# Sixteen word offsets for the split tiles of a float32r FFN, and a pad ahead of its second input

## The chip, the core and the metric

The kernel runs on one core of a Trainium2 chip. The metric is the device time of one execution in microseconds; before the change it is 880.83 us, the median of two runs (879.86 and 881.8).

## What is computed

One transformer block with attention and FFN in parallel, on x of shape (2, 2048, 256) in float32:

```python
xn = layernorm(x)
q, k, v = xn @ Wq, xn @ Wk, xn @ Wv
attn = softmax(where(causal, q @ k.T, -max) * 256 ** -0.5) @ v @ Wo
h = silu(xn @ w1.T * s1) * (xn @ w2.T * s2)      # 256 -> 1024
h = gelu(h @ h1.T * sh1)                         # 1024 -> 1024
h = gelu(h @ h2.T * sh2)                         # 1024 -> 1024
out = x + attn + h @ w3.T * s3                   # 1024 -> 256
```

The FFN's weights w1, w2, h1, h2 and w3 are ternary (-1, 0 or 1); the scales are vectors.

## The kernel before

**Stages.** The 4096 rows are cut into N = 8 blocks of TB = 512. Attention comes first and takes until about 285 us. It leaves two things in DRAM: xn of each block, transposed and split in two (`xT_d`), and the attention's result (`r_d`). Beside it, the ternary matrices are looked at, and the factors of h1 are made. A branch on `flag` then takes `ffn_ternary` (L671), which runs to the end; the other branch, `ffn`, is for weights that are not ternary and isn't run here.

**Splitting.** TensorE multiplies in the type float32r, which keeps fewer bits than float32. A value is therefore held as two float32r tiles side by side, the rounded value and the rest. `split` (L695) makes such a tile of [P, 2, TB], 4096 bytes per partition, from a pool of 16 buffers (`hp`, L678): ScalarE casts f into half 0 (L698), VectorE subtracts half 0 from f into half 1 (L699). Every product runs over both halves, `a` in (0, 1), and adds both into one PSUM bank. As the weights are small whole numbers, they need no such split.

**The FFN** takes two blocks at a time, four pairs in all. In each pair:

- `first` (L702) multiplies w1 and w2 with xn. The even block's xn lies in `xh0`, the odd block's in `xh1` (name xh1t). There are 16 steps of 8 matmuls (L715), each w [128 x 128] stationary and xn [128 x 512] moving. ScalarE takes silu (L720), VectorE multiplies (L721), and some of the results are split.
- `square` (L747) is called twice, for h1 and for h2. It is a Strassen-Winograd product: the 1024 x 1024 layer on two blocks is cut in 2 x 2, and seven products of half size stand for eight. `STEPS` (L39) names, for each, the factor of the weights and the set of four split tiles. `product` (L753) loads the factor from DRAM into one of three buffers of `wp`, and issues 4 x 4 x 2 = 32 matmuls (L763), w [128 x 128] stationary and a half of a split tile [128 x 512] moving. VectorE, ScalarE and GpSimd form the sums, the gelus and the next split tiles beside it.
- The output (L856 to L879), for the odd block and then for the even: `rest` gets `r_d` by DMA and x by another, added on GpSimd (L861). Then for each of four row tiles 16 matmuls (L871), now with the split tile [128 x 128] stationary and w3 [128 x 256] moving. VectorE scales (L877) and adds `rest` (L878) in a tile `y` of the pool `op` (L679, three buffers), and SP's queue stores it (L879).

**Order.** A scheduler places each engine's instructions when the program is built; within an engine they run in that order. SP's queue issues all the FFN's DMAs. The eight PSUM banks rotate through one pool. Pools are laid out in SBUF one after another in the order in which they are opened: first `const` with w1_sb, w2_sb, xh0, s3, the scales and `flag` (L113 to L118), then, once attention's pools are closed, `fwt` (w3_sb, xh1t), `wpt`, `stgpt`, `rawpt`, `hpt` and `opt`.

**Addresses in the built program**, in bytes in the partition, and what is left of them modulo 64: w1_sb 16512 (0), w2_sb 24704 (0), xh0 32896 (0), w3_sbt 42272 (32), xh1t 50464 (32), the three buffers of `wp` 58656, 66848 and 75040 (all 32), the 16 split tiles 150816 and on in steps of 4096 (all 32), attention's k, q, v and pT (all 32), wvo 48704 (0). A half of a split tile (2048 bytes), a column slice of w (512) and a c of xh (4096) are multiples of 64, so that these remainders hold for every operand.

Of the kernel before, what the change touches and what calls it, by code (L numbers as in the profile page):

```python
# [9 lines left out]
F32 = mybir.dt.float32  # L10
F32R = mybir.dt.float32r
# [9 lines left out]
P = 128  # L21
TB = 512
# [14 lines left out]


STEPS = [("A11", "B11"), ("S1", "T1"), ("S2", "T2"), ("S4", "B22"), ("S3", "T3"), ("A12", "B21"), ("A22", "T4")]  # L39
LOW_BITS = 0xFFF  # L40


# [20 lines left out]
def attn_ffn_kernel(  # L63
# [46 lines left out]
    const = ctx.enter_context(tc.tile_pool(name="const", bufs=1))  # L110
# [5 lines left out]
    s3 = const.tile([P, D], F32, name="s3")  # L116
    sc = {k: const.tile([P, HC], F32, name=f"{k}_s_sb") for k in ("w1", "w2", "h1", "h2")}
    flag = const.tile([1, 1], I32, name="flag")  # L118


    HB = H // 2
    HK = HC // 2
    factors = {k: dram.tile([P, len(STEPS), HK, HB], F32, name=f"factors_{k}") for k in ("h1", "h2")}

# [33 lines left out]
    with ExitStack() as actx:  # L158
# [311 lines left out]
        def score_steps(n, t):  # L470
            order = list(range(n - n % NB, n + 1))
            return [
                (6 * (TB if m < n else (t + 1) * P), lambda m=m: score(n, t, m, order))
                for m in order
            ]
# [41 lines left out]
        def look(src, dst):  # L517
            got = []

            def bits():  # L520
# [4 lines left out]
                with tc.issue_after(marks["DVE"]):  # L525
                    nc.vector.tensor_scalar(tb, tb, LOW_BITS, None, ALU.bitwise_and)
                with tc.issue_after(marks["ACT"]):
# [114 lines left out]
        while until < len(tiles) - 1:  # L642
# [7 lines left out]
            a = []  # L650
            if j < len(tiles):
                a = score_steps(*tiles[j])
                if j == 0:
                    a = []
            a = a + extra.get(j, [])
# [15 lines left out]
    def ffn_ternary(actx):  # L671
# [4 lines left out]
        stgp = actx.enter_context(tc.tile_pool(name="stgpt", bufs=2))  # L676
        rawp = actx.enter_context(tc.tile_pool(name="rawpt", bufs=25))
        hp = actx.enter_context(tc.tile_pool(name="hpt", bufs=4 * HK))  # L678
        op = actx.enter_context(tc.tile_pool(name="opt", bufs=3))  # L679
        ps = actx.enter_context(tc.tile_pool(name="pst", bufs=8, space=PSUM))  # L680

        w3_sb = fw.tile([P, HC, D], F32R, name="w3_sbt")
# [9 lines left out]
        def raw(name):  # L692
            return rawp.tile([P, TB], F32, tag="raw", name=name)

        def split(f, name):  # L695

            r = hp.tile([P, 2, TB], F32R, tag="h", name=f"h_{name}")
            nc.scalar.copy(r[:, 0, :], f)  # L698
            nc.vector.tensor_tensor(r[:, 1, :], f, r[:, 0, :].bitcast(F32), ALU.subtract)  # L699
            return r  # L700

        def first(n):  # L702
# [3 lines left out]
            for k in ("B11", "B12", "B22", "B21"):  # L706
                xh = xh1 if k[2] == "2" else xh0
                for i in range(HK):
                    o = i + (HK if k[1] == "2" else 0)
                    name = f"w_{n}_{k}_{i}"  # L710
                    p1, p2 = banks(name, 2)
                    for p, w in ((p1, w1_sb), (p2, w2_sb)):
                        for c in range(DC):
                            for a in range(2):
                                nc.tensor.matmul(  # L715
                                    out=p, lhsT=w[:, c, ts(o, P)], rhs=xh[:, c, a, :],
                                    start=(c == 0 and a == 0), stop=(c == DC - 1 and a == 1),
                                )
                    f = B[k][i] = raw(f"f_{name}")
                    nc.scalar.activation(f, p1, AF.Silu, scale=sc["w1"][:, o : o + 1])  # L720
                    nc.vector.scalar_tensor_tensor(  # L721
                        f, p2, sc["w2"][:, o : o + 1], f, ALU.mult, ALU.mult
                    )
                    if k == "B11":
                        sets[k].append(split(f, f"{n}_{k}_{i}"))
                    elif k == "B12":
                        t1(B, sets, f"{n}", i)
                    elif k == "B22":
                        b22(B, sets, f"{n}", i)
                if later and k in ("B11", "B12"):  # L730
                    later.pop(0)()
# [3 lines left out]
        def t1(B, sets, name, i):  # L735
            nc.vector.tensor_tensor(B["B11"][i], B["B12"][i], B["B11"][i], ALU.subtract)
            sets["T1"].append(split(B["B11"][i], f"{name}_T1_{i}"))

        def b22(B, sets, name, i):
            sets["B22"].append(split(B["B22"][i], f"{name}_B22_{i}"))  # L740
            nc.gpsimd.tensor_tensor(B["B12"][i], B["B22"][i], B["B12"][i], ALU.subtract)  # L741
            nc.vector.tensor_tensor(B["B22"][i], B["B22"][i], B["B11"][i], ALU.subtract)  # L742
# [4 lines left out]
        def square(layer, n, B, sets, last):  # L747
# [5 lines left out]
            def product(step, out, start):  # L753
                left, right = STEPS[step]
                w = wp.tile([P, HK, HB], F32R, tag="w", name=f"w_{name}_{left}")
                nc.sync.dma_start(
                    out=w.bitcast(F32).rearrange("p c o -> p (c o)"),
                    in_=factors[layer][:, step].rearrange("p c o -> p (c o)"),
                )
                for o in range(HK):  # L760
                    for c in range(HK):
                        for a in range(2):
                            nc.tensor.matmul(  # L763
                                out=out[o], lhsT=w[:, c, ts(o, P)], rhs=sets[right][c][:, a, :],
                                start=(start and c == 0 and a == 0), stop=(c == HK - 1 and a == 1),
                                skip_group_check=True,
                            )
                if later and step in (0, 2, 4, 5):
                    later.pop(0)()
# [77 lines left out]
        for n in range(0, N, 2):  # L847
# [8 lines left out]
            for m in (n + 1, n):  # L856
# [5 lines left out]
                h = sets["B11"] + sets["B21"] if m == n else sets["B12"] + sets["B22"]  # L862
# [164 lines left out]

    some = nc.values_load(flag[0:1, 0:1], min_val=0, max_val=LOW_BITS * SC * P)
    with tc.If(some == 0) as cmp:
        with ExitStack() as fctx:  # L1030
            ffn_ternary(fctx)
# [43 lines left out]
```

## Time and profile before

| | |
|---|---|
| median of the runs | 880.83 us |
| the profiled execution: time, and its span | 885.32 us, 883.4 us |
| granted TensorE clock, mean over the span | 0.992 |
| DVE, ACT, POOL busy | 70%, 56%, 29% |
| PE busy, its weight loads | 97%, 82% |
| start of the first L715, end of the last L871 | 285.6 us, 875.4 us |
| matmuls of L763, L715, L871 | 1792, 512, 512 |
| ACT cast L698, DVE subtract L699, x288 each | 0.62 us, 0.68 us (up to 2.8 us) |
| store of y, from issue to landing, x32 | 1.7 to 4.5 us, median 2.0 |

The span is from the first instruction of the profiled execution to its last. Busy time of PE counts a matmul from its start to its modelled end; neighbouring matmuls overlap, so that 97% doesn't say how fast they follow each other. That is read from the starts in the timeline, where a run of like instructions has one line with the start of the first, and the next line's start ends it.

### The profile page before, as it was taken

The numbers are of one execution on the slowest core, as the hardware profiler recorded it, in microseconds if no ns is written. First come the engines' busy times: TensorE is split into PE (matmuls) and PEld (weight loads), VectorE is DVE, ScalarE is ACT, GpSimd is POOL, SyncE is SP. The second block draws the span as 40 slices with busy tenths as digits, with TensorE's granted clock in tenths as the row PEclk, the third lists the DMA queues.
The fourth block names the chain that finished last, engine by engine and source line by source line (L and its number), as shares of the span: only waits on it lengthen the run. The fifth ranks groups of instructions, "written<-read, shape, count | busy, mean of one in ns | idle before, by whom it ended". The sixth has DMA issues, their size and how long they took to land.

```text
span 883.4 us, 12258 instructions
## 1 busy us (share of the span) xinstructions
PE 855.4 (97%) x4280; PEld 721.5 (82%) x4280; DVE 621.6 (70%) x1111; ACT 498.1 (56%) x881; POOL 258.4 (29%) x192
## 2 busy tenths in 40 slices
PE   8999889999998999999999999999999999999996
PEld 5988678888887878788988888888888898888886
DVE  6698667787763896786497596559568648848663
ACT  3456545755544655677256576626657635657670
POOL 4012835323211384440133051024115011502401
PEclk9999999999999999999999999999999999999999
DMA  8676699987882979844434444433444443144412
GB/s 268 243 224 200 195 313 298 343 298 207 294 253 58 377 256 343 294 143 143 137 102 144 143 143 144 155 109 118 143 142 144 143 144 96 48 143 144 143 48 76
DMA packets 63989, 162.51 MB, mean 184 GB/s; under 512 B 6704, under 2 KB 36528, under 8 KB 54704
## 3 DMA queue, kind: packets, MB, share of 16 engines
q1 hardware_dynamic: 60176, 149.07, 50.3%
q10 hardware_dynamic: 3744, 12.58, 5.0%
q8 instruction: 36, 0.59, 0.3%
q14 instruction: 33, 0.27, 0.1%
HBM read 113.92 MB, written 47.71 MB: 183 GB/s over the span
## 4 chain that ended last, share of the span: by engine, by line
PE 61%; DMA 4%; DVE 1%; POOL 1%; issue 0%; SPq 0%; POOLq 0%; DVEq 0%
PE ps_h_X L763 26%; PE ps_h_Z L763 13%; PE ps_w_B L715 10%; PE ps_h_Y L763 7%; PE ps_y L871 6%; DMA xt<-in_attn_x 2%; DMA w_h_A<-factors_h 1%; POOL rt L861 1%; DMA rt<-r_d 0%; DVE f_w_B L742 0%; DVE h_B L699 0%; POOL f_w_B L741 0%; DMA out<-yt 0%; DVE yt L878 0%; DVE yt L877 0%
## 5 line engine op out<-in xcount | busy, mean ns | idle before, releaser
L364 PE MATMUL pss<-k,q 128*128 128x512 f32 (+3 forms) x480 | 109.6, 369 | 3.7 <-ACT q L214 2.4
L364 PEld LDWEIGHTS pss<-k,q 128*128 128x128 f32 x480 | 82.3, 190 | 17.2 <-ACT q L214 2.7
L763 PE MATMUL ps_h_X<-h_h_T,w_h_S 128*128 128x512 f32 x384 | 89.0, 389 | 0.0
L443 PE MATMUL po<-v,pT 128*128 128x512 f32 x272 | 80.4, 407 | 6.5 <-ACT pT L423 5.8
L763 PEld LDWEIGHTS ps_h_X<-h_h_T,w_h_S 128*128 128x128 f32 x384 | 72.1, 188 | 15.0
L861 POOL TENSOR_TENSOR rt<-rt,xt 128x1024 f32<-128x1024 f32 x8 | 19.2, 2400 | 218.7 <-DMA rt<-r_d 212.1
L425 POOL TENSOR_TENSOR pT<-e,pT 128x512 fp32r<-128x512 f32 (+3 forms) x30 | 36.9, 1230 | 116.5 <-ACT pT L423 78.7
L784 ACT ACTIVATE k_h_u<-k_h_u,h_s_sb 128x512 f32<-128x512 f32 x64 | 46.3, 723 | 40.9 <-DVE k_h_u L783 40.7
L720 ACT ACTIVATE f_w_B<-ps_w_B,w_s_sb 128x512 f32<-128x512 f32 x64 | 43.0, 684 | 42.5 <-PE ps_w_B L715 42.5
L871 PEld LDWEIGHTS ps_y<-w_sbt,h_h_B 128*128 128x128 f32 x512 | 62.0, 192 | 0.3
L871 PE MATMUL ps_y<-w_sbt,h_h_B 128*128 128x256 f32 x512 | 62.1, 283 | 0.0
L715 PE MATMUL ps_w_B<-xh,w_sb 128*128 128x512 f32 x256 | 59.7, 390 | 1.3 <-DVE r L462 1.3
L715 PE MATMUL ps_w_B<-xh1t,w_sb 128*128 128x512 f32 x256 | 60.7, 397 | 0.0
L443 PEld LDWEIGHTS po<-v,pT 128*128 128x128 f32 x272 | 48.1, 192 | 15.0 <-ACT pT L423 6.7
L763 PE MATMUL ps_h_Y<-h_h_B,w_h_A 128*128 128x512 f32 x256 | 59.5, 389 | 0.6 <-DMA w_h_A<-factors_h 0.6
L763 PE MATMUL ps_h_X<-h_h_T,w_h_A 128*128 128x512 f32 x256 | 59.3, 389 | 0.0
L715 PEld LDWEIGHTS ps_w_B<-xh1t,w_sb 128*128 128x128 f32 x256 | 48.1, 188 | 12.0 <-ACT f_w_B L720 0.4
L715 PEld LDWEIGHTS ps_w_B<-xh,w_sb 128*128 128x128 f32 x256 | 47.8, 188 | 11.4 <-issue 1.5
L763 PEld LDWEIGHTS ps_h_Y<-h_h_B,w_h_A 128*128 128x128 f32 x256 | 48.0, 188 | 10.9 <-issue 1.0
L741 POOL TENSOR_TENSOR k_h_u<-k_h_p,k_h_u 128x512 f32<-128x512 f32 x16 | 24.3, 1526 | 110.0 <-ACT h_h_B L698 97.6
L763 PEld LDWEIGHTS ps_h_X<-h_h_T,w_h_A 128*128 128x128 f32 x256 | 48.1, 188 | 10.0
L385 ACT ACTIVATE s<-s,low 128x1024 f32<-128x1024 f32 (+7 forms) x48 | 43.0, 897 | 21.9 <-DVE low L379 21.8
(139 smaller groups left out, 1869.9 us busy)
## 6 DMA issues: line engine op xcount, KB each, us to landing
w_h_S<-factors_h SPq DMA_DIRECT2D x32, 1024.0 KB, 4.8
w_h_A<-factors_h SPq DMA_DIRECT2D x24, 1024.0 KB, 4.9
d<-b SPq DMA_DIRECT2D x18, 512.0 KB, 3.5
e<-d SPq DMA_DIRECT2D x72, 128.0 KB, 4.0
xT_d<-k SPq DMA_DIRECT2D x8, 1024.0 KB, 5.3
stg<-in_ffn_h_w ACTq DMA_DIRECT2D x16, 512.0 KB, 6.3
x<-in_attn_x SPq DMA_DIRECT2D x16, 256.0 KB, 5.3
r_d<-r SPq DMA_DIRECT2D x8, 512.0 KB, 5.8
```

The lines of the kernel that those rows point to most:

```text
L364: nc.tensor.matmul(out=ps[:, :w], lhsT=qs[n][:, c, a, ts(t, P)], rhs=ks[m][:, c, b, :w], start=(k == 0), stop=(m < n and k == 3 * DC - 1),)
L385: marks["ACT"] = nc.scalar.activation(st["s"][:, at], st["s"][:, at], AF.Exp, bias=low, accum_out=st["sums"][:, u // UK : u // UK + 1],).ins
L425: engine.tensor_tensor(lo, src, hi.bitcast(F32), ALU.subtract)
L443: nc.tensor.matmul(out=st["po"], lhsT=pT[:, 0, ts(j, P)], rhs=vs[m][:, j, :, :], start=(m == first and j == 0), stop=False,)
L715: nc.tensor.matmul(out=p, lhsT=w[:, c, ts(o, P)], rhs=xh[:, c, a, :], start=(c == 0 and a == 0), stop=(c == DC - 1 and a == 1),)
L720: nc.scalar.activation(f, p1, AF.Silu, scale=sc["w1"][:, o : o + 1])
L741: nc.gpsimd.tensor_tensor(B["B12"][i], B["B22"][i], B["B12"][i], ALU.subtract)
L763: nc.tensor.matmul(out=out[o], lhsT=w[:, c, ts(o, P)], rhs=sets[right][c][:, a, :], start=(start and c == 0 and a == 0), stop=(c == HK - 1 ...
L784: nc.scalar.activation(C[k][o], r[o] if r else banks[o], AF.Gelu, scale=s[:, at : at + 1])
L861: nc.gpsimd.tensor_tensor(rest, rest, xt, ALU.add)
L871: nc.tensor.matmul(out=ys[t][:, :D], lhsT=h[c][:, a, ts(t, P)], rhs=w3_sb[:, c, :], start=(c == 0 and a == 0), stop=(c == HC - 1 and a == 1),)
```

## The change

Three edits. A tile of 8 words per partition is added to the `const` pool, after `flag`. A split tile's buffer becomes 16 words longer, 4160 bytes, and the two halves lie in it from word 0, 1, 2, ... 15, 0, ... on, counted over all splits. The pool `op` has two buffers instead of three, which gives `y` two; `rest` and `xt` have one each by their own setting.

```diff
+SHIFTS = 16
...
     flag = const.tile([1, 1], I32, name="flag")
+    const.tile([P, 8], F32, name="pad")
...
-        op = actx.enter_context(tc.tile_pool(name="opt", bufs=3))
+        op = actx.enter_context(tc.tile_pool(name="opt", bufs=2))
...
+        splits = [0]
+
         def split(f, name):

-            r = hp.tile([P, 2, TB], F32R, tag="h", name=f"h_{name}")
+            t = hp.tile([P, 2 * TB + SHIFTS], F32R, tag="h", name=f"h_{name}")
+            r = t[:, ds(splits[0] % SHIFTS, 2 * TB)].rearrange("p (a t) -> p a t", a=2)
+            splits[0] += 1
             nc.scalar.copy(r[:, 0, :], f)
             nc.vector.tensor_tensor(r[:, 1, :], f, r[:, 0, :].bitcast(F32), ALU.subtract)
             return r
```

In the built program of the change w1_sb, w2_sb and xh0 stay where they were. Everything after `const` moves: w3_sbt, xh1t, the three buffers of `wp`, the 16 split buffers (now in steps of 4160), k, q, v and pT begin at a multiple of 64, wvo at 32 past one. A split tile's two halves lie at its word offset past a multiple of 64. PE, ACT, POOL and SP have the same instructions in the same order; on VectorE, L877 and L878 of the later output tiles of a pair stand one to three places further back.

## The prediction

> **What bounds the kernel now.** I read the share of each engine first, then the chain that ended last, then the waits of PE in the FFN, then the starts of its matmuls in the timeline. The share and the chain on the page:
>
> ```profile
> PE 855.4 (97%) x4280; PEld 721.5 (82%) x4280; DVE 621.6 (70%) x1111; ACT 498.1 (56%) x881; POOL 258.4 (29%) x192
> ...
> PE ps_h_X L763 26%; PE ps_h_Z L763 13%; PE ps_w_B L715 10%; PE ps_h_Y L763 7%; PE ps_y L871 6%; DMA xt<-in_attn_x 2%; DMA w_h_A<-factors_h 1%; POOL rt L861 1%; DMA rt<-r_d 0%; DVE f_w_B L742 0%; DVE h_B L699 0%; POOL f_w_B L741 0%; DMA out<-yt 0%; DVE yt L878 0%; DVE yt L877 0%
> ```
>
> 62% of the span stands on the chain as FFN matmuls (26+13+10+7+6). The waits of PE between 294 and 884 us are two, both in the first pair of blocks:
>
> ```profile
> PE ps_h_X L763 <- DVE f_w_B L721: 2.2, 1, 2.2
> PE ps_h_Y L763 <- DMA w_h_A<-factors_h: 0.6, 1, 0.6
> ```
>
> So from 285.6 us (first L715) to 875.4 us (end of L871) PE waits 2.8 us for anything with a name, and the FFN's time is the number of its matmuls times the distance from one start to the next. That distance, not the mean duration (389 ns at L763, which overlaps), is the number to read. Timeline of PE, second pair of blocks; the columns are start in us, length in us, engine, line:
>
> ```profile
> 443.03 15.15 PE L715 MATMUL ps_w_B<-xh1t,w_sb 128*128 128x512 f32 x64
> 458.02 7.44 PE L715 MATMUL ps_w_B<-xh,w_sb 128*128 128x512 f32 x32
> 465.30 7.46 PE L763 MATMUL ps_h_X<-h_B,w_h_A 128*128 128x512 f32 x32
> 472.60 7.42 PE L763 MATMUL ps_h_Z<-h_T,w_h_S 128*128 128x512 f32 x32
> ```
>
> Starts differ by 14.99 us for the 64 matmuls on xh1t: 234.2 ns each. The 32 on xh take 7.28 us: 227.5 ns. The chain of work has the products of L763 at 7.25 us each throughout, 226.6 ns a matmul. These are matmuls of one size, none waiting. What differs is the place of the operands. In the built program w1, w2 and xh0 start at a multiple of 64 bytes; xh1t, the split tiles and the factors in wp all start 32 bytes (8 words) past one. Moving and stationary operand are therefore 0 words apart (modulo 16) at L763 and in L715 on xh, and 8 apart in L715 on xh1t. Apart by 0, 226.6 to 227.5; apart by 8, 234.2.
>
> Apart by 0 isn't enough, though. In attention k and q are also 0 apart, yet runs of 12 that wait for nothing go slower:
>
> ```profile
> 200.01 2.93 PE L364 MATMUL pss<-k,q 128*128 128x512 f32 x12
> 202.78 0.64 PE L448 MATMUL po<-v,pT 128*128 128x256 f32 x4
> ...
> 228.85 2.91 PE L364 MATMUL pss<-k,q 128*128 128x512 f32 x12
> 231.60 0.39 PE L443 MATMUL po<-v,pT 128*128 128x512 f32 x1
> ```
>
> 2.77 and 2.75 us for 12: 230.8 and 229.2 ns. Read start by start, such runs step irregularly between 224 and 240 ns, while L763 after at most some ten irregular steps repeats 227, 227, 226 to its end. I read this as settling: where every pair of operands has the same offset, the starts fall into a rhythm at 226.6; where not, they wander at 230 to 234.
>
> **What the Trainium skill says.** "TensorE: Matmul & The Clock Gate", Back-to-back issue gap, prices a warm matmul at N/2.4+2.5 ns, 215.8 for 512 columns; this trace shows 226.6 at best over a product, 10.8 more. The same page (Part 2, step 1) says that PE has two separate SBUF read ports, so that loading the next weights doesn't steal bandwidth from the running matmul; 234.2 against 227.5 for an offset alone speaks against full independence. "SBUF — State Buffer", Operand start alignment, lets a 4-byte operand start at any word and says of it "This is about legality, not speed". So the 16 words are allowed and unpriced. Its Specifications give 16-byte cachelines with a penalty for each crossing; no run here shows it.
>
> **The change part by part.** On PE, ACT, POOL and SP the instructions and their order are the same; on DVE only the last output tiles of each pair move. What changes is addresses.
>
> 1. *The pad* moves everything after the const pool by 32 bytes. xh1t comes to 0 apart from w1 and w2: 256 matmuls (64 in each of four pairs) from 234.2 to 227.5, 6.7 ns each: -1.7 us. In attention q, k, v and pT move together and wvo stays 8 words from k: nothing.
>
> 2. *The split tiles at L763.* The factors are now at 0 and the r-th split lies at word r mod 16. A pair's splits come in sets of four, so a product of 32 matmuls meets four neighbouring offsets, two matmuls each, and over the products all 16 come about equally often. The trace prices two of the sixteen: 0 (226.6) and 8 (234.2). Straight between them around the circle, the mean distance from 0 is 4 words, which gives 230.4. The runs that never settle give 229 to 231 at offset 0 itself. I take 231: 4.4 ns by 1792 matmuls (14 products of 32 in each pair, four pairs) = +7.9 us. Bounds: below, 224, the shortest step seen, -4.7 us; above, all at 234.2, +13.6 us.
>
> 3. *The split tiles at L871* are the stationary operand, 256 columns. Starts are 119.9 ns apart (420.54 to 435.89 us for 128). pv in attention, 8 apart, 24 of 256 columns from 195.37 to 198.25 us, has 120.0. Nothing; at best about -1 us (512 by 2 ns).
>
> 4. *Writing them.* The 288 splits (72 a pair) are an ACT cast (620 ns) and a DVE subtract (680 ns undisturbed). No such write off a 32-byte boundary is in the trace. During the products DVE is busy 66% (252.9 of 381 us in four windows), so a slower write hides there; before the first product it is busy 92% (24.78 of 27 us). Below: nothing, since the amount of data is equal. Above: 10% on 16 subtracts there, 1.1 us in each pair, +3 us after the first pair. I take 0.
>
> 5. *Two y buffers instead of three.* L877 of tile 2 now waits for tile 0 to be stored. The end of the kernel:
>
> ```profile
> 875.50 1.09 DVE L878 TENSOR_TENSOR yt<-yt,rt 128x256 f32<-128x256 f32 x3 [1.52 <-POOL rt L861]
> 875.95 3.24 SPq L879 DMA_DIRECT2D out<-yt  x4
> 877.78 0.42 DVE L877 TENSOR_TENSOR yt<-ps_y,s 128x256 f32<-128x256 f32 x1 [1.19 <-DMA out<-yt]
> 878.23 0.42 DVE L878 TENSOR_TENSOR yt<-yt,rt 128x256 f32<-128x256 f32 x1
> ```
>
> POOL ends the sum of rest late, three L878 follow, and tile 3 waits for tile 0's store until 877.78. After the change tile 2 waits for that same store and tile 3 for the next: four DVE operations instead of two stand after 877.78, +2 x 0.43 = +0.9 us, on the path that sets the end. At the three earlier pair ends the same wait holds L721 of the next pair behind it on DVE, and so the PSUM banks that L715 wants; two or three banks are still free there and PE shows no wait, so nothing; without that cover 3 x 0.9 us.
>
> Sum: -1.7 + 7.9 + 0 + 0 + 0.9 = +7.1 us. The profiled execution has a span of 883.4 us and a time of 885.32, so span 890.5; against the median of 880.83 us, 4.5 below that execution's time, 887.9.
>
> **Rivals.** *A, the rhythm holds whatever the offset.* Neighbouring offsets shift a start by a word (0.4 ns), which the rhythm may absorb. For it: after waits, L763 always returned to 226.6. Against: xh1t never does in 64 matmuls. Time: 880.83 - 1.7 + 0.9 = 880.0. *B, faster: other offsets keep the two reads out of each other's way.* For it: 10.8 ns a matmul over the skill's price have to come from something, and steps of 224 exist. Against: in the runs read they are single steps followed by long ones. At 224: 880.0 - 4.7 = 875.3. It turns faster than before where L763 falls below 227. More than 2% (17.6 us) would need 217.3. *C, over 2% slower: starts inside a 32-byte group cost more than any offset seen.* Place: 14 of 16 offsets at L763. Price: at 240, the longest step seen, 13.4 ns by 1568 = +21 us, 901. It decides from a mean of 236.9 at L763. Against: moving words are consecutive wherever they begin.
>
> **How the numbers follow.** The wandering rhythm 0.57, with its own range 884 to 894 (L763 at 228.8 to 234.2); A 0.17; B 0.16; C 0.10. Forecast 888. The range 874 to 897 holds the first, A, most of B, and part 4 at its upper bound; C lies outside. Over 2%, about what a measurement of this kernel can tell from no change: slower 0.10 (C), faster 0.03 (the far end of B), within 0.87.
>
> **What would show it.** Right: xh1t's 64 in 14.6 us; products of 7.3 to 7.5 us instead of 7.25, longer for sets whose words lie near 8; y's last L877 later by 0.9 us. Wrong: products all at 7.25 (A), below (B), or above 7.6 (C); L699 longer than 0.68 us where POOL is idle; a new PE wait at L715.

## The result and the profile after

The changed kernel takes 893.56 us (median of 893.36 and 893.75) against 880.83 us: ratio 1.0144, 95% interval 1.0095 to 1.0194, 12.7 us more (8.4 to 17.1). Its profiled execution has a time of 893.36 us and a span of 891.6 us.

From the page of the changed kernel, the share of PE and the chain that ended last (L721, L769 and L877 are before's L715, L763 and L871, six lines down):

```profile
PE 862.8 (97%) x4280; PEld 720.4 (81%) x4280; DVE 621.5 (70%) x1111; ACT 498.2 (56%) x881; POOL 257.6 (29%) x192
...
PE ps_h_X L769 27%; PE ps_h_Z L769 13%; PE ps_w_B L721 12%; PE ps_h_Y L769 7%; PE ps_y L877 6%; DMA e<-d 4%; PE pss L366 4%; PE po L445 3%; DMA d<-b 2%; PE pv L338 2%; SPq L269 2%; PE po L450 1%; DMA stg<-in_ffn_h_w 1%; DMA x<-d_x 1%; PE pq L322 1%
```

The instruction counts are as before and the busy times of the other engines within 1.1 us; PE alone is busy 7.4 us longer. Its waits between 280 and 895 us are two: 1.8 us for L727 at the first product, and 1.3 us at the first L721. The kernel before has both as well (2.2 and 1.3 us). So there is no new wait, and again the starts have to be read. Timeline of PE, second pair of blocks:

```profile
440.73 15.09 PE L721 MATMUL ps_w_B<-xh1t,w_sb 128*128 128x512 f32 x64
455.66 7.43 PE L721 MATMUL ps_w_B<-xh,w_sb 128*128 128x512 f32 x32
462.94 7.61 PE L769 MATMUL ps_h_X<-h_B,w_h_A 128*128 128x512 f32 x32
470.38 7.60 PE L769 MATMUL ps_h_Z<-h_T,w_h_S 128*128 128x512 f32 x32
477.82 2.48 PE L769 MATMUL ps_h_X<-h_T,w_h_S 128*128 128x512 f32 x10
```

The two products take 7.44 us each (470.38 - 462.94, 477.82 - 470.38), 232.5 ns a matmul, where before had 7.25. xh1t's 64 take 14.93 us, 233.3 ns, where 227.5 was expected.

The end of the changed kernel:

```profile
880.92 0.76 DVE L884 TENSOR_TENSOR yt<-yt,rt 128x256 f32<-128x256 f32 x2 [3.42 <-POOL rt L867]
881.37 6.04 SPq L885 DMA_DIRECT2D out<-yt  x4
883.22 0.42 DVE L883 TENSOR_TENSOR yt<-ps_y,s 128x256 f32<-128x256 f32 x1 [1.54 <-DMA out<-yt]
885.81 0.42 DVE L883 TENSOR_TENSOR yt<-ps_y,s 128x256 f32<-128x256 f32 x1 [2.17 <-DMA out<-yt]
886.15 0.75 DVE L884 TENSOR_TENSOR yt<-yt,rt 128x256 f32<-128x256 f32 x2
```

Two waits for stores stand where before had one, and the second is the longer: the second store came back at 885.81, some 4 us after its issue. From the last matmul's end (880.83) to the end of the span (891.56) it is 10.7 us; before, 7.9 (875.43 to 883.38).

**Where the 12.7 us are.** Between the first L721 and the end of the span, the trace of the changed kernel is 11.6 us longer than that of the kernel before. The 14 products of a pair take 2.0 us more in the first pair (before had lost 0.6 us there to a wait for a factor) and 2.8, 2.9 and 2.8 us more in the others; in the second it is 104.38 us against 101.59. Together that is 10.5. Over four pairs L721 is 0.8 us shorter and L877 0.8 us shorter, and the end is 2.8 us longer. The measured 12.7 us agree with this within their interval.

The two spans differ by 8.2 us only, since attention ended at 282.2 us in this trace and at 285.6 in that of before. Over all profiles of this study that point lies anywhere from 281.3 to 288.9 us. The change doesn't make this spread: up to the branch all thirteen built programs have the same instructions in the same order, and the eight with a pad of 24 words, from 281.3 to 286.9 us, have the same addresses there too. So I compare runs by their ratios and stages by their own lengths.

### The profile page after: what moved, and what is told of

The parts are those of the page before. It is cut to its first block, busy times and chain, and to the rows that moved or that the text cites. A ratio compares the mean times of both kernels' runs of the same rounds, so it can differ in the third digit from the quotient of the medians.

```text
span 891.6 us, 12259 instructions
## 1 busy us (share of the span) xinstructions
PE 862.8 (97%) x4280; PEld 720.4 (81%) x4280; DVE 621.5 (70%) x1111; ACT 498.2 (56%) x881; POOL 257.6 (29%) x192
## 4 chain that ended last, share of the span: by engine, by line
PE 77%; DMA 11%; DVE 4%; issue 3%; SPq 2%; POOL 1%; ACT 1%; POOLq 0%; DVEq 0%; ACTq 0%
PE ps_h_X L769 27%; PE ps_h_Z L769 13%; PE ps_w_B L721 12%; PE ps_h_Y L769 7%; PE ps_y L877 6%; DMA e<-d 4%; PE pss L366 4%; PE po L445 3%; DMA d<-b 2%; PE pv L338 2%; SPq L269 2%; PE po L450 1%; DMA stg<-in_ffn_h_w 1%; DMA x<-d_x 1%; PE pq L322 1%
## 5 line engine op out<-in xcount | busy, mean ns | idle before, releaser
L769 PE MATMUL ps_h_X<-h_h_T,w_h_S 128*128 128x512 f32 x384 | 91.5, 395 | 0.0
L769 PEld LDWEIGHTS ps_h_X<-h_h_T,w_h_S 128*128 128x128 f32 x384 | 72.5, 189 | 17.1
L877 PEld LDWEIGHTS ps_y<-w_sbt,h_h_B 128*128 128x128 f32 x512 | 61.1, 188 | 0.3
L877 PE MATMUL ps_y<-w_sbt,h_h_B 128*128 128x256 f32 x512 | 61.2, 281 | 0.0
L769 PE MATMUL ps_h_X<-h_h_T,w_h_A 128*128 128x512 f32 x256 | 61.0, 395 | 0.0
L769 PE MATMUL ps_h_Y<-h_h_B,w_h_A 128*128 128x512 f32 x256 | 61.0, 395 | 0.0
L721 PE MATMUL ps_w_B<-xh,w_sb 128*128 128x512 f32 x256 | 59.6, 390 | 1.3 <-DVE r L464 1.3
L721 PE MATMUL ps_w_B<-xh1t,w_sb 128*128 128x512 f32 x256 | 60.4, 394 | 0.0
L769 PEld LDWEIGHTS ps_h_X<-h_h_T,w_h_A 128*128 128x128 f32 x256 | 48.3, 189 | 11.3
L769 PEld LDWEIGHTS ps_h_Y<-h_h_B,w_h_A 128*128 128x128 f32 x256 | 48.3, 189 | 11.3
L721 PEld LDWEIGHTS ps_w_B<-xh1t,w_sb 128*128 128x128 f32 x256 | 47.9, 187 | 11.7
L721 PEld LDWEIGHTS ps_w_B<-xh,w_sb 128*128 128x128 f32 x256 | 47.8, 188 | 11.4 <-issue 1.5
```

Source lines behind the costliest of these rows:

```text
L721: nc.tensor.matmul(out=p, lhsT=w[:, c, ts(o, P)], rhs=xh[:, c, a, :], start=(c == 0 and a == 0), stop=(c == DC - 1 and a == 1),)
L769: nc.tensor.matmul(out=out[o], lhsT=w[:, c, ts(o, P)], rhs=sets[right][c][:, a, :], start=(start and c == 0 and a == 0), stop=(c == HK - 1 ...
L877: nc.tensor.matmul(out=ys[t][:, :D], lhsT=h[c][:, a, ts(t, P)], rhs=w3_sb[:, c, :], start=(c == 0 and a == 0), stop=(c == HC - 1 and a == 1),)
```

## The experiments

The theory on record (M16) counts the distance between moving and stationary operand modulo 16 words; M32 and M64 below count it modulo 32 and 64. V says that only a distance that varies inside a product costs, L that the length of the buffers does. The 233.3 ns of xh1t, which the change puts 0 apart modulo 16 but 16 apart modulo 32 and 48 modulo 64, spoke against M16. All ratios are to the kernel before, with a 95% interval. Its median beside these runs was 884.8 to 885.4 us. From the first map on, all kernels but the changed one with three y buffers have the pad of 24 words; the diffs leave it out.

**The pad alone.**

```diff
+    const.tile([P, 8], F32, name="pad")
```

> The kernel before with the pad of 8 words alone: three y buffers, split tiles 0 words from the factors, xh1t 16 words (64 bytes) from w1 and w2. Theory M16 (the prediction's: distance counts modulo 16 words): xh1t is 0 apart, its 64 matmuls take 14.56 us (227.5 ns), 1.7 us less over the kernel. Theory M32 (distance counts modulo 32 words, since the profile after shows xh1t at 233.3 ns): its 64 take 14.93 us as there, 0.2 us less over the kernel. Both: the products of L763 stay at 7.25 us, the end after the last matmul at 8.0 us. A third reading, that 64-byte alignment alone slows attention, would put some us on the first stage.

**A pad of 24 words instead.**

```diff
+    const.tile([P, 24], F32, name="pad")
```

> The kernel before with a pad of 24 words instead of 8, which puts everything after it, xh1t too, at a multiple of 128 bytes, as w1 and w2 are. Both M16 and M32: xh1t's 64 matmuls take 14.56 us (227.5 ns), 1.7 us less over the kernel, products of L763 at 7.25 us. If xh1t stays at 233 ns, both are wrong and the period is longer still, 64 words or more. Against the pad of 8 words: equal under M16, 1.5 us faster under M32.

Measured: 8 words 0.9997 (0.9975 to 1.0019), 24 words 0.9967 (0.9950 to 0.9983). Timeline of PE, second pair, first with 8 words, then with 24:

```profile
445.60 15.09 PE L716 MATMUL ps_w_B<-xh1t,w_sb 128*128 128x512 f32 x64
460.54 7.43 PE L716 MATMUL ps_w_B<-xh,w_sb 128*128 128x512 f32 x32
467.81 7.43 PE L764 MATMUL ps_h_X<-h_B,w_h_A 128*128 128x512 f32 x32
475.07 7.42 PE L764 MATMUL ps_h_Z<-h_T,w_h_S 128*128 128x512 f32 x32
```

```profile
440.75 14.67 PE L716 MATMUL ps_w_B<-xh1t,w_sb 128*128 128x512 f32 x64
455.25 7.42 PE L716 MATMUL ps_w_B<-xh,w_sb 128*128 128x512 f32 x32
```

xh1t takes 14.94 us with 8 words and 14.50 with 24 (226.6 ns a matmul). M16 falls: with 8 words xh1t lies 0 from w1 modulo 16 and stays slow. With either pad the products stay at 7.26 us, so moving both operands together by 32 or 96 bytes costs nothing. The pad of 24 words is faster than the kernel before by 2.9 us (1.5 to 4.4), of which the starts of L715 (29.04 us a pair against 29.57) show 2.1.

**Two y buffers alone.**

```diff
-        op = actx.enter_context(tc.tile_pool(name="opt", bufs=3))
+        op = actx.enter_context(tc.tile_pool(name="opt", bufs=2))
```

> The kernel before with two y buffers instead of three, nothing else. The prediction's step 5: 0.9 us later at the end (four DVE operations instead of two behind the returned store). The profile after (10.8 us from the last matmul to the end against 8.0): 2.8 us, as the second store lands late. At the three earlier pair ends nothing: PE shows no new wait.

Measured: 1.0028 (1.0011 to 1.0045), 2.5 us (1.0 to 4.0). Its end in the trace:

```profile
876.94 0.76 DVE L878 TENSOR_TENSOR yt<-yt,rt 128x256 f32<-128x256 f32 x2 [3.44 <-POOL rt L861]
877.40 3.95 SPq L879 DMA_DIRECT2D out<-yt  x4
879.24 0.94 DVE L877 TENSOR_TENSOR yt<-ps_y,s 128x256 f32<-128x256 f32 x2 [1.54 <-DMA out<-yt]
880.09 0.75 DVE L878 TENSOR_TENSOR yt<-yt,rt 128x256 f32<-128x256 f32 x2
```

Here the second store was back in time: L877 runs twice in a row, and after the returned store stand four operations until 880.84 where before has two, close to the 0.9 us predicted. In two other traces with two buffers, the changed kernel's and the first map's, the second store came back late, and the end was 2.8 and 2.6 us later. In the ten traces with three buffers the span ends 7.4 to 8.1 us after the last matmul; with two buffers 8.7 us here, 10.7 and 10.5 in those two. Which of the two an execution gets isn't settled; the median of 2.5 us suggests that the late store is common.

**First map: one word per set.**

```diff
-        op = actx.enter_context(tc.tile_pool(name="opt", bufs=3))
+        op = actx.enter_context(tc.tile_pool(name="opt", bufs=2))
...
+            t = hp.tile([P, 2 * TB + 32], F32R, tag="h", name=f"h_{name}")
+            r = t[:, ds(splits[0] // HK % 32, 2 * TB)].rearrange("p (a t) -> p a t", a=2)
...
```

> A map: the four split tiles of a set all lie at the same word, the next set one word further, 0 to 31 and round again; buffers of 4096 + 128 bytes and a pad of 24 words, so that word r is r words from the factors modulo 32. Each product is then 32 matmuls at one distance. M16: words 0 and 16 settle at 226.7 ns (7.25 us a product), the rest wander at 230 to 234. M32: only word 0 settles there; word 16 stands at 233 as xh1t does after. A third theory, V (it is the varying of the offset inside a product that costs): every word settles at 226.7. Two y buffers, so some 2.8 us at the end; whole kernel 885 to 893 under M16 and M32, 881 to 884 under V.

Measured: 892.76 us in one run, which lies in the range of M16 and M32. But word 0 stood at 231.7 ns and no other word settled at 226.7, which neither foresaw. The buffers, in steps of 4224 bytes, lie alternately 0 and 32 words from the factors modulo 64. If 32 words made no difference, word 0 would have settled. xh1t with the pad of 24, which does settle, lies 0 from w1 modulo 64 (64 modulo 128). So the period that fits is 64 words, 256 bytes (M64); the next map tests it.

**Second map: the factors moved instead.**

```diff
...
+                wt = wp.tile([P, HK * HB + 64], F32R, tag="w", name=f"w_{name}_{left}")
+                flat = wt[:, ds(products[0] % 64, HK * HB)]
+                products[0] += 1
...
```

> A second map, cleaner than the first, whose buffers in steps of 4224 bytes let two distances 32 words apart take turns inside each product: split tiles as before in steps of 4096 bytes, pad of 24 words, three y buffers, and the factor of each product one word further into its buffer, 0 to 55. Every product is 32 matmuls at one constant distance; the 56 products have the distances 0 and 9 to 63 words modulo 64. Theory M64 (distance counts modulo 64 words, 256 bytes): only distance 0 settles at 226.7 ns (7.25 us a product), 40 stands at 234.2 and 48 at 233.3 as xh1t did before and after, the rest 228 to 239. M32: 32 settles at 226.7 too. M16: 16, 32 and 48 too. V (only variation inside a product costs): all settle at 226.7. If any distance stands below 226, the offsets could gain something.

Measured: 893.07 us in one run. Timeline of PE, products 23 to 27 of the map (the first is 0), distances 41 to 37:

```profile
533.95 7.62 PE L770 MATMUL ps_h_X<-h_h_T,w_h_S 128*128 128x512 f32 x32
541.40 7.65 PE L770 MATMUL ps_h_Z<-h_h_B,w_h_S 128*128 128x512 f32 x32
548.89 7.42 PE L770 MATMUL ps_h_X<-h_h_T,w_h_S 128*128 128x512 f32 x32
556.15 7.62 PE L770 MATMUL ps_h_Y<-h_h_B,w_h_A 128*128 128x512 f32 x32
563.61 7.53 PE L770 MATMUL ps_h_X<-h_h_T,w_h_A 128*128 128x512 f32 x32
```

Next starts minus starts: 7.45, 7.49, 7.26, 7.46 us. Read start by start, each product falls into a cycle of its own, one to eleven steps that repeat to its end. Mean of the cycle in ns, by distance:

```
0: 226.7   9: 233.3  11: 236.7  16: 228.9  23: 237.3  25: 226.7  28: 226.7  31: 226.7
32: 233.3  34: 226.7  37: 230.0  39: 226.7  40: 234.3  48: 233.3  49: 230.0   most others: 233.3
mean over the 56: 232.3; lowest 226.7
```

M16 and M32 fall again (16, 32 and 48 don't stand at 226.7), and so does V: the distance is constant inside each product, and most are slow. M64 holds in its main point, and 40 and 48 give the very numbers of xh1t before (234.2) and after (233.3). Its rider, that distance 0 alone settles at 226.7, is wrong: 25, 28, 31, 34 and 39 do too. No distance in this map is better than 0, so none of them would have gained anything at the products.

**The buffers' length alone.**

```diff
-            r = hp.tile([P, 2, TB], F32R, tag="h", name=f"h_{name}")
+            t = hp.tile([P, 2 * TB + 16], F32R, tag="h", name=f"h_{name}")
+            r = t[:, : 2 * TB].rearrange("p (a t) -> p a t", a=2)
```

> One part of the change alone: the split tiles' buffers are 4160 bytes long as in the change, but every tile lies at word 0 of its buffer; pad of 24 words, three y buffers. The four tiles of a set then lie 0, 16, 32 and 48 words from the factors modulo 64, in turn. M16: all the same distance, products at 7.25 us, 880 us or 2 to 3 us under the kernel before, as with the pad alone. M64: the length alone brings the tiles off distance 0, products at 7.35 to 7.45 us (230 to 233 ns), +6 to +11 us on the pad alone, so that most of the change's cost would come from the 64 bytes added to each buffer and not from the 16 words.

Measured: 1.0027 (1.0010 to 1.0044), so 0.6% or 5.3 us over the pad alone. Timeline of PE, the first products of the second pair:

```profile
467.60 7.65 PE L765 MATMUL ps_h_X<-h_B,w_h_A 128*128 128x512 f32 x32
475.09 7.58 PE L765 MATMUL ps_h_Z<-h_T,w_h_S 128*128 128x512 f32 x32
482.50 7.58 PE L765 MATMUL ps_h_X<-h_T,w_h_S 128*128 128x512 f32 x32
```

Products are as M64 says, 231.7 ns on average (7.49 and 7.41 us for the first two here). 64 bytes more in each buffer are enough to lose the rhythm, with every tile at word 0. At the output, though, 256 columns took 117.5 ns a start instead of 119.9, and 115.6 where the distance was 16 or 32.

**The changed kernel with three y buffers.**

```diff
-        op = actx.enter_context(tc.tile_pool(name="opt", bufs=2))
+        op = actx.enter_context(tc.tile_pool(name="opt", bufs=3))
```

> The changed kernel with three y buffers as before, nothing else. By the run of the kernel before with two (ratio 1.0028, some 2.5 us) and the profile after (2.8 us more between the last matmul and the end): 2.5 to 2.8 us less than the changed kernel, products unchanged at 7.45 us, 8.0 us from the last matmul to the end. By the prediction's step 5, 0.9 us less.

Measured: 1.0098 (1.0075 to 1.0121), some 4 us less than the changed kernel's 1.0144. The intervals overlap, so the size isn't settled by this alone; but its 0.98% and the 0.28% of the two buffers alone add up to 1.26%, 11.1 us, near the 11.6 of the traces. In its trace the end is 7.6 us after the last matmul (882.81 to 890.4), and the products still take 233.2 ns a matmul.

**The 16 words alone, in turn and by sets.** Buffers in steps of 4352 bytes, so that the length brings no distance of its own; the second kernel has `splits[0] // HK % 16`.

```diff
-        rawp = actx.enter_context(tc.tile_pool(name="rawpt", bufs=25))
+        rawp = actx.enter_context(tc.tile_pool(name="rawpt", bufs=23))
...
+            t = hp.tile([P, 2 * TB + 64], F32R, tag="h", name=f"h_{name}")
+            r = t[:, ds(splits[0] % 16, 2 * TB)].rearrange("p (a t) -> p a t", a=2)
+            splits[0] += 1
...
```

> The 16 words alone: split tiles at word 0 to 15 in turn, as in the change, but in buffers in steps of 4352 bytes (a multiple of 256), so that a tile at word r is exactly r words from the factors modulo 64; pad of 24 words, three y buffers, two buffers fewer for the float32 values to make room. Against the pad alone (226.7 ns at L763). Theory M64: 231 to 234 ns, +8 to +13 us, as the change has it. Theory L (it was the length of the buffers that cost): near 226.7.

> As the run with the 16 words alone, but the four tiles of a set share one word, and the next set has the next; the same 16 distances, each constant inside its product. Theory M64 as the second map has it: each distance has its own rhythm, 0 at 226.7, 9 and 12 at 233.3, 11 at 236.8, 14 at 230.5, and the same numbers come out although here the split tiles are moved and there the factors were. If distance between the two operands isn't what counts, the numbers differ. Theory V (variation inside a product costs by itself): the mean over all products stands well under that of the run with words in turn, by 3 ns or more; if only the distance counts, within 1 ns of it.

Measured: both 1.0062 (1.0037 to 1.0086, and 1.0038 to 1.0087), so 0.95% or 8.4 us over the pad alone, by the two intervals some 6 to 11. The products of the second pair are 2.7 and 2.8 us longer than with the pad alone (104.29 and 104.33 us against 101.55), by four 11 us, so the runs settle the direction better than the size. The two buffers fewer for float32 values aren't the cause: PE's waits are 2.3 and 2.6 us at the first product and 1.3 at the first L720, against 2.2 and 1.3 in the kernel before. Timeline of PE with the words in turn, second pair:

```profile
463.70 7.61 PE L768 MATMUL ps_h_X<-h_B,w_h_A 128*128 128x512 f32 x32
471.15 7.59 PE L768 MATMUL ps_h_Z<-h_T,w_h_S 128*128 128x512 f32 x32
478.58 3.66 PE L768 MATMUL ps_h_X<-h_T,w_h_S 128*128 128x512 f32 x15
```

After the first product, the starts are 232.9 ns apart with the words in turn and 233.2 by sets. L falls, since the words cost without the length, and V falls, since it makes no difference whether the offset varies inside a product. Chain of the kernel by sets, products at the words 1, 3, 2, 4 and 5:

```profile
322.89 7.58 PE ps_h_Z L768 x32
330.46 7.36 PE ps_h_X L768 x32
337.82 7.41 PE ps_h_Z L768 x32
345.24 7.42 PE ps_h_X L768 x32
352.65 7.68 PE ps_h_Y L768 x32
```

The means of the settled cycles, read start by start, in ns. Each word has three or four products, and all of one word agree, but for word 9, once at 240.0, and 2 and 12, once lower:

```
0: 226.7   1: 236.7   2: 233.3   3: 230.0
4: 231.6   5: 240.0   6: 235.0   7: 230.0
8: 233.3   9: 235.0  10: 235.0  11: 230.0
12: 233.3  13: 236.7  14: 232.0  15: 228.3
```

The columns differ: words 1, 5, 9 and 13 are the highest of their rows (9 level with 10), 3, 7, 11 and 15 the lowest after 0. The first map, read the same way, has the columns too, up to word 31: 235 to 239 at one past a multiple of 4, 228 to 232 at three past. But of the seven distances that the second map shares with this kernel (9 to 15), six stand elsewhere there, where the factors were moved: 11 stands at 230.0 here and at 236.7 there. So M64's second claim fails: between offsets that aren't multiples of 8 words the distance alone doesn't fix the rhythm; where each operand starts counts as well. The second map has one product for each distance, and the way in which a product starts can pick its cycle too, as the words 9, 2 and 12 show; but that is too rare here to explain six of seven.

**Another distance at the output.** w3 moved into a longer tile, 16 or 32 words on, with the pad of 24.

```diff
+        w3_t = fw.tile([P, HC * D + 64], F32R, name="w3_sbt")
+        w3_sb = w3_t[:, ds(16, HC * D)].rearrange("p (c d) -> p c d", c=HC)
```

> The kernel before with the pad of 24 words, and w3 moved 16 words into a longer tile, so that at the output w3 (moving, 256 columns) and the split tiles (stationary) lie 16 words apart instead of 0; all other distances stay 0. The run with longer buffers had 115.6 ns a start there at distances 16 and 32 and 119.9 at 0. Theory M64 with a rhythm for each distance: 113 to 118 ns, the 128 matmuls of a pair in 14.5 to 15.1 us instead of 15.35, 1 to 3.5 us less than with the pad alone over the four pairs, so 3.5 to 6 us under the kernel before. Rival: the 115.6 came from the mixture of distances, and a constant 16 stands at 120 as 0 does: no change against the pad alone.

> As the run with w3 16 words off, but 32 words off. Theory M64: 113 to 118 ns a start at the output, 1 to 3.5 us less than with the pad alone. Theory M32, if it held for 256 columns: 32 is the same as 0, 119.9 ns, no change. Rival of the mixture: 120 ns.

Timeline of PE with 16:

```profile
422.25 15.24 PE L873 MATMUL ps_y<-w_sbt,h_h_B 128*128 128x256 f32 x128
437.33 7.44 PE L717 MATMUL ps_w_B<-xh,w_sb 128*128 128x512 f32 x32
```

128 matmuls in 15.08 us, 117.8 ns, 1.1 us less in four pairs; with 32, 15.36 us, 120.0 ns, no gain. So 16 is a little better and 32 equal, and the 115.6 came from the mixture. Ratios: 0.9942 (0.9916 to 0.9968) and 0.9948 (0.9932 to 0.9965). Both beat the kernel before and the changed one; that 16 beats the pad of 24 alone (0.9967) is shown by the starts, not by the runs.

## Why the prediction was right, and where not

The direction and the place were right: slower, at the starts of L763, with no new wait, inside the range (893.56 in 874 to 897). Forecast +7.1 us, measured +12.7. What it said of the kind, a rhythm that is lost, was right only in part.

1. *The pad, -1.7: wrong.* The failing step is "modulo 16". The period is 64 words, the pad leaves xh1t 48 from w1, and its matmuls went from 234.2 to 233.3 ns only (-0.3 us over its 256). A pad of 24 words does what was forecast.
2. *The split tiles at L763, +7.9: right in place, too small, and not by wandering.* Measured +10.5. The mis-sized term is the mean interval, 231 against 233.0 (104.38 us over 448 matmuls). "Straight between them around the circle" was wrong: 234.2 at 8 apart was taken for the peak, but 8 words stand at 233.3, an ordinary value, and 1 and 5 words at 236.7 and 240.0. And the tiles lay elsewhere than assumed: with the buffers in steps of 4160 bytes the distances modulo 64 are 0, 4, 8, 12, 19, ... 61, not 0 to 15. The forecast sign, longer products for sets near word 8, didn't come: sets at the words 8 to 11 stood at 232.5 ns, those at 0 to 3 at 235.0 in 13 of 14 products. Nor was the length of the buffers priced: alone it makes 231.7 ns, the words alone 232.9, both together 233.0, so the two don't add.
3. *At L871, 0, at best -1:* -0.8.
4. *Writing them, 0: right.* The subtracts of the split are 676 to 682 ns at their shortest, as before (672 to 680), and DVE is busy 621.5 us, before 621.6.
5. *Two y buffers, +0.9: right in mechanism, too small.* The four operations cost about that where both stores return alike. The prediction had no term for a second store that returns later than the first; with it the end is 2.8 us longer in the changed kernel's trace, and the runs of this edit alone say 2.5. No new PE wait arose at the earlier pair ends, as said.

*Wandering was a misreading.* From short runs of attention the prediction took it that a distance of 0 isn't enough, and that without equal offsets the starts wander. Read to their ends, k and q settle as well: the run at 228.85 us steps by 231, 236, 228, 233, 230 ns and then by 227, 227, 226 to its end, and one at 190.93 us is there from its first step. These runs are short, and L763 shows the same irregular steps after a wait. Nor does xh1t wander: in the kernel before it repeats seven steps (235, 235, 233, 232, 237, 238, 230) up to its 64th matmul, and in the changed kernel 55 of the 56 products repeat eight. So each arrangement of addresses has a rhythm of its own, and most are slower than that of 0. The forecast of a slower L763 came true although its reason, the mixing of offsets inside a product, wasn't needed: constant distances cost as much.

Rival A (the rhythm absorbs the offsets) fails at products of 7.44 us and B (faster) at 226.7 being the lowest of all settled cycles at L763. C's mechanism exists, starts off a 32-byte boundary up to 240.0, but its mean of 236.9 wasn't reached.

What stays open: what in the two reads collides. That it is the load of the next stationary operand against the moving one is an inference from the distances; no run has the one without the other. Nor is it shown what the remaining 10.8 ns are over the 215.8 that the Trainium skill ("TensorE: Matmul & The Clock Gate", Back-to-back issue gap) gives for an isolated matmul of 512 columns.

## What to carry to other kernels

Where TensorE is the bound, read start to start from the timeline and compare like matmuls: a few ns, the same to the end of a run, are no wait and name no releaser, but 6 ns over 1792 matmuls are some 11 us. A short run says little: read it to its end, and look for the cycle. If moving and stationary tiles both lie at the same place modulo 256 bytes here, leave them there, and count the length of a buffer as part of the address of the next. A buffer taken away to make room is a change of its own: here it was about a fifth of the loss (2.5 of 12.7 us), at the end of the kernel, where nothing hides it.

## What the runs showed of the hardware

- 128x512 float32r matmuls, each with its own 128x128 stationary operand: 226.7 to 240.0 ns between starts in a settled run, by the addresses of the operands alone. The steps repeat in a cycle, of one to eleven where the distance is constant; after a break it took some ten irregular steps, or fewer, to reach it. Means of 226.7, 230.0, 233.3, 236.7 and 240.0 recur; they differ by multiples of 3.33 ns.
- The period of that effect is 256 bytes, seen at the offsets that are multiples of 32 bytes; moving both operands together by 32 or 96 bytes changed nothing.
- With the words by sets, a moving operand one word past a multiple of 16 bytes was slowest (235.0 to 240.0), three words past fastest (228.3 to 230.0) of those not at 0; moving the stationary operand instead gave no such pattern. The Trainium skill ("SBUF — State Buffer", Specifications) has cachelines of 16 bytes; the pattern of four words agrees in size, but no run shows that they are its cause.
- Of the four stores of y issued one after another at the end, the first was back after 1.8 us; the second took about 4 us in two of the three traces with two buffers.
